# The first stage's projection on eight 64x32 tiles, its gram on column halves and its gate on four strips at once

## The chip, the cores and the metric

One Trainium2 chip, of which the kernel uses one core. The metric is the device time of one execution in microseconds (us), from start to end on the chip.

## The reference

Two layers work on an image x of 4 x 64 x 256 x 256 (batch, channels, height, width), all in fp32. Layer 0 is a channel-attention block with a convolutional feed-forward part; layer 1 is a linear attention along rows, one along columns and a two-layer perceptron. The change touches the start of layer 0 only. Cut to that:

```python
h = layernorm(x, ln1_w, ln1_b)              # over the 64 channels of a pixel
proj = conv1x1(h, in_proj_w)                # 64 -> 64 channels
local, glob = split(proj, 2, axis=1)        # 32 + 32 channels
qkv = dwconv3x3(conv1x1(glob, qkv_w), qkv_dw)
q, k, v = split(qkv, 3)                     # 4 heads of 8 channels each
g = sigmoid(conv1x1(relu(conv1x1(glob, gate_w1, gate_b1)), gate_w2, gate_b2))
dk = clip(floor(8 * g.mean()), 1, 8)        # one number from all pixels
attn = einsum(l2norm(q), l2norm(k))         # 8 x 8 per head, summed over all pixels
attn = softmax(where(attn >= kth_largest(attn, dk), attn, -inf))
```

So the stage needs three things of every pixel: its projection (kept for later), its share of the products of q and k (the gram, summed over all pixels of an image) and its gate value (summed over everything). The local half goes on to a branch of its own (`_lgce` in the reference: a 1x1 convolution, a channel weight from the image's means, and two sigmoids).

## The kernel before

The kernel is one program written in stages, and every engine runs its instructions in the order of the program. The stage that is changed, `stage_a`, walks over 4 images of 16 strips; a strip is 16 image rows, and a pass of the loop over n is called a step here. A step works on several strips at once, through generators that `_steps` advances in turn: `pairs` for strip n-3, `proj` for strip n-1, `norm` for strip n, and in every second step of images 1 to 3 also `local` for the image before. `gate` runs ahead of them, for strip n-2.

- `norm` transposes the strip on PE from channels on partitions to pixels on partitions (L520), ACT copies that out of PSUM into `xp` (L521), and `layernorm` (L311 to L321) runs on DVE and ACT: a sum, a subtraction, a square on ACT (L314), a sum, a square root on ACT (L318), a reciprocal, a product.
- `proj` transposes the result back (L540, copied out on DVE at L541), so that 128 partitions hold the 64 channels of an even and of an odd row ("parity"), and multiplies by `win` (L547), a 128x128 matrix that has the 64x64 weights of either parity on its diagonal and zeros elsewhere. ACT adds the bias and writes `pj` (L549), which goes to DRAM (L556). The gate's hidden layer follows, on four tiles of 32 columns (L559), with its relu on DVE (L561).
- `pairs` brings `pj` into `gp`, four image rows on 128 partitions, by SBUF-to-SBUF DMAs (L577 to L585), convolves to q and k of two rows at once by three accumulated matmuls (L604), DVE copies that into `qT` (L609), and the gram adds qT times qT (L595, 128x128, of which only the two 64x64 blocks on the diagonal are read, at L637 and L638).
- `gate` multiplies the hidden layer of one strip by the second gate weights (L566), and ACT takes the sigmoid and its sum (L568).
- `local` is two groups of 32x32 tiles (L462), ACT evictions (L466, L470), a product on DVE (L472) and a sigmoid on ACT (L473).

An fp32 matmul of the source stands in the trace as two LDWEIGHTS and two MATMULs. Tiles of PSUM come from `mm()`, a ring of six banks that all parts of the stage share in the order of the program; the gram has one of two `sm()` banks. ACT must load a table when it changes between sigmoid (L470, L473, L568) and square root (L318).

The constants come from `_prep` as packs, one DMA each: pack "a" has `win`, `g2T` (second gate weights, one 16x8 matrix per strip part, of which 8 columns are used) and their biases. After stage_a come the last image's `local`, the attention weights, and the later stages, which the change does not touch.

Of the kernel before, what the change touches and what calls it, by code (L numbers as in the profile page):

```python
# [22 lines left out]
def _prep(a):  # L23
# [7 lines left out]
    def put(name, v, rows=None):  # L31
        v = np.asarray(v, f)
        P[name] = grp, v.reshape(v.shape[0] if rows is None else rows, -1)
# [8 lines left out]
    def col(v, n):  # L42
        return np.tile(np.asarray(v).reshape(-1), n)[:, None]
# [14 lines left out]
    for par in (0, 1):  # L58
        for lg in (0, 1):
            win[par, :, lg, par, :] = wi[lg * 32:(lg + 1) * 32].T  # L60
    put("win", win, 128)
    put("ln1w", col(L0["ln1_w"], 2))
    put("ln1b", col(L0["ln1_b"], 2))
    qkv, dwq = L0["qkv_w"], L0["qkv_dw"][:, 0]
# [16 lines left out]
        g1[64 + par * 32:96 + par * 32, par, :] = L0["gate_w1"].T  # L81
    put("g1T", g1)
    put("g1b", col(L0["gate_b1"], 8))
    g2 = np.zeros((8, 16, 8), f)
    for i in range(8):
        g2[i, :, i] = L0["gate_w2"][0]
    put("g2T", g2, 128)
    put("g2b", col(L0["gate_b2"], 8))


    grp = "l"
# [4 lines left out]
    put("spb", col(np.repeat(L0["cbam_spb"][:, 0], 4), 4))  # L96
    put("gmask", p[:, None] % 32 // 4 == p[None, :] % 32 // 4)
    grp = "s"
    put("ones8", np.ones((8, 32)))
    put("fold", (p[:, None] % 64 == np.arange(64)[None, :]))  # L100
    put("hb", (p[:32, None] // 8 == p[None, :32] // 8))
    put("vA", qkv[64:])
# [145 lines left out]
def kernel(ctx: ExitStack, tc: tile.TileContext, x, packs, fd, out, off):  # L248
# [77 lines left out]
    p1 = sp1.enter_context(tc.tile_pool(name="pst1", bufs=1))  # L326
    KL = load_pack(p1, "l")
    sumA = p1.tile([128, B], F32, name="sumA")
    gsum = p1.tile([8, B, 16], F32, name="gsum")
    gram2 = [p1.tile([128, 64], F32, name=f"gram{b}") for b in range(B)]  # L330
    wc = [const.tile([128, 3, 64], F32, name=f"wc{b}") for b in range(B)]
    cw = [p1.tile([128, 1], F32, name=f"cw{b}") for b in range(B)]
# [10 lines left out]
    def attention_weights():  # L343
        vt = p1.tile([32, 12, 32], F32, name="vt")
        V.tensor_tensor(vt, mid_bc(K("vA"), 12), bc(K("vD"), 32), ALU.mult)

        gs = p.tile([8, 1], F32, name="gs")
        V.tensor_reduce(gs, gsum.rearrange("p a b -> p (a b)"), AX.X, ALU.add)
        t = mm()
        T.matmul(t[:32, 0:1], K("ones8"), gs, start=True, stop=True)  # L350
        dk = p1.tile([32, 1], F32, name="dk")
        V.tensor_scalar(dk, t[:32, 0:1], 8.0 / (B * HW), 1.0, ALU.mult, ALU.max)
        asc = p1.tile([32, 1], F32, name="asc")
        V.tensor_reduce(asc, K("asc"), AX.X, ALU.add)
        for b in range(B):

            t = mm()
            T.matmul(t[:64, :64], K("fold"), gram2[b], start=True, stop=True)
            gm = p.tile([64, 64], F32, name="gm")
            V.tensor_copy(gm, t[:64, :64])  # L360
            dg = p.tile([64, 64], F32, name="dg")
            V.tensor_tensor(dg, gm, ident[:64, :64], ALU.mult)
            n2 = p.tile([64, 1], F32, name="n2")
            V.tensor_reduce(n2, dg, AX.X, ALU.add)
            nr = p.tile([64, 1], F32, name="nr")
            V.tensor_scalar(n2, n2, 1e-24, None, ALU.max)
            S.activation(nr, n2, AF.Sqrt)
            ri = p.tile([64, 1], F32, name="ri")
            V.reciprocal(ri, nr)
            n1 = p.tile([64, 64], F32, name="n1")  # L370
            V.tensor_scalar(n1, gm, ri, None, ALU.mult)
            t = mm()
            T.transpose(t[:64, :64], n1, ident[:64, :64])
            nn = p.tile([64, 64], F32, name="nn")
            V.tensor_scalar(nn, t[:64, :64], ri, None, ALU.mult)
            am = p.tile([32, 32], F32, name="am")
            V.tensor_tensor(am, nn[0:32, 32:64], K("hb"), ALU.mult)
            at = p.tile([32, 8], F32, name="at")
            V.tensor_reduce(at, am.rearrange("p (h d) -> p d h", h=4), AX.X, ALU.add)
            V.tensor_scalar(at, at, K("temp"), None, ALU.mult)  # L380

            gt = p.tile([32, 8, 8], F32, name="gt")
            V.tensor_tensor(gt, mid_bc(at, 8), bc(at, 8), ALU.is_gt)
            kp = p.tile([32, 8], F32, name="kp")
            V.tensor_reduce(kp, gt, AX.X, ALU.add)
            V.tensor_scalar(kp, kp, 1.0, dk, ALU.add, ALU.is_le)
            mx = p.tile([32, 1], F32, name="mx")
            V.tensor_reduce(mx, at, AX.X, ALU.max)
            V.tensor_scalar(at, at, mx, None, ALU.subtract)
            ex = p.tile([32, 8], F32, name="ex")  # L390
            S.activation(ex, at, AF.Exp)
            V.tensor_tensor(ex, ex, kp, ALU.mult)
            sx = p.tile([32, 1], F32, name="sx")
            V.tensor_reduce(sx, ex, AX.X, ALU.add)
            rx = p.tile([32, 1], F32, name="rx")
            V.reciprocal(rx, sx)
            V.tensor_scalar(ex, ex, rx, asc, ALU.mult, ALU.mult)
            pb = p.tile([32, 4, 8], F32, name="pb")
            V.tensor_tensor(pb, mid_bc(ex, 4), K("hb").rearrange("p (h d) -> p h d", h=4), ALU.mult)

            t = mm()
            T.matmul(t[:32, :64], pb.rearrange("p h d -> p (h d)"), K("opgT"), start=True, stop=True)
            eb = p.tile([32, 64], F32, name="eb")
            V.tensor_copy(eb, t[:32, :64])
            t = mm()
            for i in range(3):
                T.matmul(t[:, i * 64:(i + 1) * 64], vt[:, i * 4:(i + 1) * 4, :].rearrange("p a c -> p (a c)"), eb, start=True, stop=True)
            V.tensor_copy(wc[b].rearrange("p a c -> p (a c)"), t[:, :192])

            V.tensor_copy(wc[b][64:96, 1, :], K("oplr")[64:96])  # L410
            yield
# [74 lines left out]
    def stage_a():  # L486
        NS = H // 16
        with tc.tile_pool(name="pa", bufs=2) as pa, tc.tile_pool(name="pa1", bufs=1) as pk:
            K = load_pack(pk, "a")

            win = pk.tile([128, 128], F32, name="win")
            V.tensor_scalar(win, K("win"), K("ln1w"), None, ALU.mult)
            t = mm()
            T.matmul(t[:, 0:1], K("win"), K("ln1b"), start=True, stop=True)
            bin_ = pk.tile([128, 1], F32, name="bin_")
# [14 lines left out]
            def norm(b, s):  # L510

                xs = ld.pop((b, s))
                xns[b, s] = []
                for hf in (0, 1):
                    xp = pa.tile([128, 16, C], F32, name="xp")
                    for k in (0, 1):
                        tp = mm()
                        for i in range(4):
                            ii = hf * 8 + k * 4 + i
                            T.transpose(tp[:, i * 128:(i + 1) * 128], xs[:, ii // 2, (ii % 2) * 128:(ii % 2) * 128 + 128], ident)  # L520
                        S.copy(xp[:, k * 8:(k + 1) * 8, :].rearrange("p a c -> p (a c)"), tp)  # L521
                    yield
                    xn = pa.tile([128, 16, C], F32, name="xn", bufs=4)
                    layernorm(pa, xp, xn, 16)
                    xns[b, s].append(xn)
                    yield

            def proj(b, s):
# [13 lines left out]
                    xTs.append(xT)  # L542
                    yield
                for hf in (0, 1):
                    for k in (0, 1):
                        pr = mm()
                        T.matmul(pr, win, xTs[hf][:, k * 512:(k + 1) * 512], start=True, stop=True)  # L547
                        n = (s * 2 + hf) * 2 + k
                        S.activation(pj[:, hf * 4 + k * 2:hf * 4 + k * 2 + 2, :].rearrange("p a c -> p (a c)"), pr, AF.Identity,  # L549
                                     bias=bin_, accum_out=sacc[b][:, n:n + 1])  # L550
                    yield
# [5 lines left out]
                hp = mm()  # L557
                for i in range(4):
                    T.matmul(hp[i * 32:(i + 1) * 32, :], K("g1T"), pj[:, 2 * i:2 * i + 2, :].rearrange("p a c -> p (a c)"), start=True, stop=True)  # L559
                hs = pa.tile([128, 512], F32, name="hs")  # L560
                V.tensor_scalar(hs, hp, K("g1b"), 0.0, ALU.add, ALU.max)  # L561
                hss[b, s] = hs

            def gate(b, s):
                zp = mm()
                T.matmul(zp[:8, :], K("g2T"), hss.pop((b, s)), start=True, stop=True)  # L566
                gj = pa.tile([8, 512], F32, name="gj")
                S.activation(gj, zp[:8, :], AF.Sigmoid, bias=K("g2b"), accum_out=gsum[:, b, s:s + 1])  # L568

            def pairs(b, s):  # L570

# [20 lines left out]

                def acc(qT, i):
                    for k in range(4):
                        T.matmul(gram[:, :128], qT[:, k * 128:(k + 1) * 128], qT[:, k * 128:(k + 1) * 128],  # L595
                                 start=(s == 0 and i == 0 and k == 0), stop=(s == NS - 1 and i == 3 and k == 3))

                for i in range(4):
                    yield
# [17 lines left out]
            for n in range(len(seq) + 3):  # L617
                if n + 1 < len(seq):
                    ld[seq[n + 1]] = load(*seq[n + 1])
                if 0 <= n - 2 < len(seq):  # L620
                    gate(*seq[n - 2])

                m = n - NS - 2
# [10 lines left out]
                    local_weights(b)  # L634
                if n >= 3 and seq[n - 3][1] == NS - 1:
                    b = seq[n - 3][0]
                    V.tensor_copy(gram2[b][0:64], grams[b][0:64, 0:64])  # L637
                    V.tensor_copy(gram2[b][64:128], grams[b][64:128, 64:128])  # L638

    stage_a()  # L640

# [713 lines left out]
```

## Time and profile before

| | |
|---|---|
| median of 3 runs | 9063.34 us (9060.01 to 9071.98) |
| the profiled execution | 9063.4 us, span 9061.6 us |
| PE busy over the span | 8382.1 us (93%) |
| DVE, ACT busy | 5945.5 us (66%), 4740.4 us (52%) |
| stage_a's gram, L595 | 2048 MATMULs, busy 287.9 us |
| stage_a's projection, L547 | 512 MATMULs, busy 242.1 us |
| stage_a's gate, L566 | 128 MATMULs, busy 79.6 us |
| stage_a's convolution, L604 | 6144 MATMULs, busy 733.3 us |
| table loads of L568 and L318 in stage_a and just after | 60 and 87, of 1283 ns each |

Busy time is the union of the instructions of a row, and [...] consecutive matmuls overlap. The time from the start of one group of instructions to the start of the next says more about what the engine can do; the timeline view gives it. A row of the timeline has the start, the length, the engine, the line, the operation with its tiles and shapes, and in brackets the idle time before it and what ended that.

### The profile page before, as it was taken

The page shows a single profiled execution, that of the slowest core. Times are in us where ns is not written, and L with a number is a line of the kernel's source. Part 1 is how long each engine was busy: PE and PEld are TensorE (multiplying, and loading weights), DVE is VectorE, ACT ScalarE, POOL GpSimd, SP SyncE. Part 2 cuts the span into 40 slices and gives each one's busy share as a digit, 9 for nine tenths or more (in the row PEclk, how much of TensorE's full clock was granted, in tenths as well). Part 3 has the DMA queues.
Part 4 walks back from the last instruction along what each step waited for, and adds up shares of the span by engine and source line. Part 5 has one row for each costly group of instructions (what it writes and reads, how often), then busy time and mean ns, then how long its engine had stood idle before and what let it go on. Part 6 is the DMA issues. An engine that isn't in the chain of part 4 may idle for free. (4 is left out here: it accounts for less than half of the span.)

```text
span 9061.6 us, 136047 instructions
## 1 busy us (share of the span) xinstructions
PE 8382.1 (93%) x53934; PEld 4354.5 (48%) x53934; DVE 5945.5 (66%) x8509; ACT 4740.4 (52%) x7844; POOL 1135.0 (13%) x1828
## 2 busy tenths in 40 slices
PE   8999999789999998999999999999997888898897
PEld 7877777534444443333333344444453333333333
DVE  6666666467777775222222288888887778878876
ACT  4455555545555554222222266666655767766765
POOL 1111111112221221000000011111110000000000
PEclk9999999889999999999999999999998999999999
DMA  6677767599999998888888855555533233233232
GB/s 149 138 178 173 173 168 172 152 317 384 391 393 392 382 388 333 297 297 296 297 297 297 279 163 172 173 172 168 168 117 69 53 66 66 55 66 64 58 66 47
DMA packets 1258475, 1831.95 MB, mean 202 GB/s; under 512 B 335600, under 2 KB 1040112, under 8 KB 1196656
## 3 DMA queue, kind: packets, MB, share of 16 engines
q1 hardware_dynamic: 1053296, 1034.55, 37.8%
q0 software_dynamic: 204544, 788.69, 26.6%
q8 instruction: 428, 7.01, 0.3%
q14 instruction: 207, 1.70, 0.1%
HBM read 967.57 MB, written 788.53 MB: 194 GB/s over the span
## 5 line engine op out<-in xcount | busy, mean ns | idle before, releaser
L900 DVE TENSOR_TENSOR y<-ge,mm 128x512 f32<-128x512 f32 (+1 forms) x640 | 406.2, 635 | 1212.2 <-ACT ge L899 1212.2
L867 PE MATMUL mm<-t,w 128*128 128x512 f32 (+1 forms) x2560 | 1093.9, 566 | 19.6 <-DMA t<-td 19.6
L899 ACT ACTIVATE ge<-mm 128x512 f32<-128x512 f32 (+1 forms) x640 | 354.7, 554 | 1253.8 <-PE mm L874 1253.8
L1298 ACT ACTIVATE hg<-mm,b 128x512 f32<-128x512 f32 x1024 | 631.7, 685 | 332.6 <-PE mm L1296 330.7
L760 PE MATMUL mm<-gp,wc 128*64 128x510 f32 (+1 forms) x3072 | 702.0, 595 | 89.4 <-DVE xm L770 51.2
L867 PEld LDWEIGHTS mm<-t,w 128*128 128x128 f32 x2560 | 455.4, 190 | 648.1 <-issue 437.5
L604 PEld LDWEIGHTS mm<-wqk,gp 128*128 128x128 f32 x6144 | 711.6, 192 | 71.2 <-issue 42.4
L604 PE MATMUL mm<-wqk,gp 128*128 128x128 f32 x6144 | 733.3, 276 | 0.0
L1307 PE MATMUL mm<-hg,pack_d 128*64 128x512 f32 x2048 | 579.4, 609 | 100.7 <-ACT hg L1298 100.7
L1296 PE MATMUL mm<-xfT,w 64*128 64x512 f32 x2048 | 638.4, 666 | 4.8 <-ACT xfT L1285 4.2
L815 ACT COPY tb<-mm 128x512 f32<-128x512 f32 x512 | 300.2, 587 | 632.3 <-PE mm L809 632.0
L874 PE MATMUL mm<-t,w 64*64 64x504 f32 (+1 forms) x5120 | 575.6, 555 | 0.0
L809 PE MATMUL mm<-xl,pack_c 64*128 64x512 f32 x2048 | 511.8, 599 | 8.9 <-ACT xl L797 4.7
L760 PEld LDWEIGHTS mm<-gp,wc 128*64 128x64 f32 x3072 | 278.1, 137 | 468.0 <-issue 330.2
L314 ACT ACTIVATE ln_sq<-xn 128x1024 f32<-128x1024 f32 x256 | 274.4, 1072 | 347.1 <-DVE xn L312 347.0
L316 DVE TENSOR_REDUCE ln_v<-ln_sq 128x16 f32<-128x1024 f32 x256 | 311.9, 1219 | 147.2 <-ACT ln_sq L314 147.2
L955 PE MATMUL mm<-ya,pack_e 128*64 128x512 f32 x1024 | 381.1, 616 | 11.2 <-DMA ya<-yd 11.2
L1309 DVE TENSOR_SCALAR st<-mm,pack_d 128x512 f32<-128x512 f32 x256 | 279.1, 1090 | 169.8 <-PE mm L1307 169.8
L1167 ACT ACTIVATE ln_sq<-xc 128x1024 f32<-128x1024 f32 x256 | 266.9, 1055 | 219.9 <-DVE xc L1165 219.7
L813 DVE COPY tb<-mm 128x512 f32<-128x512 f32 x512 | 344.9, 685 | 22.3 <-PE mm L809 16.8
L1296 PEld LDWEIGHTS mm<-xfT,w 64*128 64x128 f32 x2048 | 220.9, 202 | 272.4 <-issue 159.5
L874 PEld LDWEIGHTS mm<-t,w 64*64 64x64 f32 x5120 | 158.1, 132 | 374.4 <-issue 374.4
(455 smaller groups left out, 15547.3 us busy)
## 6 DMA issues: line engine op xcount, KB each, us to landing
t<-td SPq DMA_DIRECT2D x256, 1152.0 KB, 10.5
td<-tb POOLq DMA_DIRECT2D x144, 1024.0 KB, 16.1
td<-tb POOLq DMA_DIRECT2D x288, 512.0 KB, 13.9
yd<-y POOLq DMA_DIRECT2D x128, 1152.0 KB, 10.1
ya<-yd SPq DMA_DIRECT2D x192, 512.0 KB, 5.7
xs<-in_x_dram SPq DMA_DIRECT2D x128, 512.0 KB, 6.7
projd<-pj POOLq DMA_DIRECT2D x256, 256.0 KB, 4.8
gp<-projd SPq DMA_DIRECT2D x128, 512.0 KB, 9.5
```

Source lines behind the costliest of these rows:

```text
L604: T.matmul(qp[:, k * 128:(k + 1) * 128], gp[:, 2 * i + k // 2, at + dx:at + dx + 128], wqk[:, dx, :], start=(dx == 0), stop=(dx == 2))
L760: T.matmul(tv[i * 64:(i + 1) * 64, :, o], wc[2 * pr + i][:, dx, :], gps[i][:, 2 * r:2 * r + 2, i_], start=(dx == 1), stop=False, skip_grou ...
L809: T.matmul(t, inT[q, hf * 128:(hf + 1) * 128], xls[b // 2, s][q, :, 2 * y:2 * y + 2].rearrange("p f y t -> p f (y t)"), start=True, stop=True)
L813: V.tensor_copy(o, i_)
L867: T.matmul(t[:, :n], w[:, 0:128], x_[:, c, :], start=True, stop=False, skip_group_check=True)
L874: T.matmul(t[po:po + 64, :n].rearrange("p (n c) -> p n c", c=64)[:, :, o], w[q:q + 64, 128:192], x_[q:q + 64, c, i_], start=False, stop=Tr ...
L899: S.activation(ge[:, :n], ts[0][k][:, :n], AF.Gelu)
L900: V.tensor_tensor(y[:, c, :].rearrange("p n c -> p (n c)"), ge[:, :n], ts[1][k][:, :n], ALU.mult)
L955: T.matmul(t[b * 64:(b + 1) * 64, :], owT, ya[:, :, 2 * r:2 * r + 2, b * 64:(b + 1) * 64].rearrange("p f y t -> p y f t"), start=True, sto ...
L1296: T.matmul(t, w1[rh * 64:(rh + 1) * 64, i * 128:(i + 1) * 128], xT[rh * 64:(rh + 1) * 64], start=True, stop=True)
L1298: S.activation(g, t, AF.Gelu, bias=b1[:, i:i + 1])
L1307: T.matmul(y[rh * 64:(rh + 1) * 64, :], w2[:, i, :], hg[i * 2 + rh], start=False, stop=(i == 1), skip_group_check=True)
```

## The change

The projection no longer multiplies by zeros. For each half strip the two banks of PSUM (k = 0, 1) are filled together by eight matmuls, each of 64 rows by 32 columns: row half r of `xT` with the weights of that parity, for the local and the global channels (lg). For the second bank the column place of the two parities is swapped, so that the eight tiles lie in eight different places of the array; to have the right parity there, `norm` writes the second half of `xp` with the two parities exchanged, by two copies in place of one. The gram is computed as two products of 64 columns, which go to partitions 0 to 63 and 64 to 127 of the same bank. The gate waits until four strips have their hidden layers and runs their four matmuls at once, each with 32 columns of weights (24 of them zero), then one sigmoid over 128 partitions.

The line attention of layer 1 is the same in both kernels.

```diff
     put("win", win, 128)
+    put("winx", win[::-1], 128)
...
-    g2 = np.zeros((8, 16, 8), f)
+    g2 = np.zeros((8, 16, 32), f)
...
-    put("g2b", col(L0["gate_b2"], 8))
+    put("g2b", col(L0["gate_b2"], 128))
...
-    put("ones8", np.ones((8, 32)))
+    put("ones8", np.tile(p[:, None] % 32 < 8, (1, 32)))
...
-    gsum = p1.tile([8, B, 16], F32, name="gsum")
+    gsum = p1.tile([128, B, 4], F32, name="gsum")
...
+            winx = pk.tile([128, 128], F32, name="winx")
+            V.tensor_scalar(winx, K("winx"), K("ln1w"), None, ALU.mult)
...
-                        S.copy(xp[:, k * 8:(k + 1) * 8, :].rearrange("p a c -> p (a c)"), tp)
+                        if k == 0:
+                            S.copy(xp[:, 0:8, :].rearrange("p a c -> p (a c)"), tp)
+                        else:
+                            for a in (0, 1):
+                                S.copy(xp[:, 8:16, :].rearrange("p (i a) c -> p a i c", a=2)[:, 1 - a], tp.rearrange("p (i a c) -> p a i c", a=2, c=C)[:, a])
...
                 for hf in (0, 1):
-                    for k in (0, 1):
-                        pr = mm()
-                        T.matmul(pr, win, xTs[hf][:, k * 512:(k + 1) * 512], start=True, stop=True)
+                    prs = [mm(), mm()]
+                    for lg in (0, 1):
+                        for r in (0, 1):
+                            for k, w in ((0, win), (1, winx)):
+                                q = lg * 64 + (r ^ k) * 32
+                                T.matmul(prs[k][q:q + 32, :], w[r * 64:(r + 1) * 64, q:q + 32], xTs[hf][r * 64:(r + 1) * 64, k * 512:(k + 1) * 512], start=True, stop=True)
+                    for k, pr in enumerate(prs):
...
-                hs = pa.tile([128, 512], F32, name="hs")
+                hs = pa.tile([128, 512], F32, name="hs", bufs=5)
...
             def gate(b, s):
                 zp = mm()
-                T.matmul(zp[:8, :], K("g2T"), hss.pop((b, s)), start=True, stop=True)
-                gj = pa.tile([8, 512], F32, name="gj")
-                S.activation(gj, zp[:8, :], AF.Sigmoid, bias=K("g2b"), accum_out=gsum[:, b, s:s + 1])
+                for i in range(4):
+                    T.matmul(zp[i * 32:(i + 1) * 32, :], K("g2T"), hss.pop((b, s - 3 + i)), start=True, stop=True)
+                gj = pa.tile([128, 512], F32, name="gj", bufs=1)
+                S.activation(gj, zp, AF.Sigmoid, bias=K("g2b"), accum_out=gsum[:, b, s // 4:s // 4 + 1])
...
                     for k in range(4):
-                        T.matmul(gram[:, :128], qT[:, k * 128:(k + 1) * 128], qT[:, k * 128:(k + 1) * 128],
-                                 start=(s == 0 and i == 0 and k == 0), stop=(s == NS - 1 and i == 3 and k == 3))
+                        for po in (0, 1):
+                            v = qT[:, k * 128 + po * 64:k * 128 + po * 64 + 64]
+                            T.matmul(gram[po * 64:po * 64 + 64, :64], v, v, start=(s == 0 and i == 0 and k == 0), stop=(s == NS - 1 and i == 3 and k == 3))
...
-                if 0 <= n - 2 < len(seq):
+                if 0 <= n - 2 < len(seq) and n % 4 == 1:
                     gate(*seq[n - 2])
...
-                    V.tensor_copy(gram2[b][0:64], grams[b][0:64, 0:64])
-                    V.tensor_copy(gram2[b][64:128], grams[b][64:128, 64:128])
+                    V.tensor_copy(gram2[b], grams[b][:, 0:64])
```

More of the change, by code (lines that the diff above doesn't have):

```diff
@@ L345, in attention_weights @@
         V.tensor_tensor(vt, mid_bc(K("vA"), 12), bc(K("vD"), 32), ALU.mult)
-        gs = p.tile([8, 1], F32, name="gs")
+        gs = p.tile([128, 1], F32, name="gs")
         V.tensor_reduce(gs, gsum.rearrange("p a b -> p (a b)"), AX.X, ALU.add)
```

## The prediction

> **What bounds the kernel now.** The page first: PE is busy for 93% of the span, and the slices put the changed stage, stage_a, into the first eight of forty, with PE at 8 or 9 tenths. Then the timeline of all engines in that stage. One step (16 image rows) starts with the transposes of line L540. In the first batch each step takes 23.5 us: L540 starts at 151.04 and again at 174.56. From L462's first use on, steps alternate, one with a piece of local() and one without; a pair takes about 54.9 us (L540 at 876.54 and 931.38). The windows of two plain steps, of a step with local() and of the 4 us after it:
>
> ```profile
> core 0: us, PE busy (x) PEld busy (x) DVE busy (x) ACT busy (x) POOL busy (x), PEclk, DMA share, GB/s
> 111.00:134.50 23.50, 23.50 (x180) 19.60 (x180) 15.90 (x21) 10.99 (x21) 2.48 (x6) 1.00 0.68 146
> 134.50:158.00 23.50, 23.50 (x180) 19.60 (x180) 15.90 (x21) 10.98 (x21) 2.47 (x6) 1.00 0.70 146
> 876.40:903.90 27.50, 25.47 (x233) 19.42 (x232) 17.07 (x19) 20.18 (x32) 6.84 (x14) 1.00 0.78 204
> 903.90:907.90 4.00, 3.59 (x11) 1.93 (x11) 1.02 (x2) 0.00 (x0) 0.00 (x0) 0.57 1.02 269
> ```
>
> A plain step is PE from end to end. A step with local() is not: ACT has 20 us of 27.5, and the timeline at its end shows PE waiting for DVE, which follows ACT:
>
> ```profile
> 901.02 1.06 PE L559 MATMUL mm<-pj,pack_a 128*32 128x512 f32 x8
> 901.80 0.31 ACT L318 ACTIVATE ln_d<-ln_v,eps_t 128x16 f32<-128x16 f32 x1
> 902.43 1.23 DVE L321 TENSOR_TENSOR xn<-xn,ln_r 128x1024 f32<-128x1024 f32 x1
> 903.57 0.68 DVE L609 COPY qT<-mm 128x512 f32<-128x512 f32 x1
> 904.31 2.08 PE L595 MATMUL sm<-qT 128*128 128x128 f32 x8 [2.23 <-DVE qT L609]
> 906.32 1.61 PE L566 MATMUL mm<-hs,pack_a 128*8 128x512 f32 x2
> ```
>
> After that wait of 2.23 us the granted clock falls (0.57 in the last window; L595's eight take 2.08 instead of 1.06 us). PE's own rows give the prices, start to start:
>
> ```profile
> 159.08 1.06 PE L595 MATMUL sm<-qT 128*128 128x128 f32 x8
> 159.97 1.88 PE L547 MATMUL mm<-xT,win 128*128 128x512 f32 x4
> 161.69 1.04 PE L520 MATMUL mm<-pack_k,xs 128*128 128x128 f32 x8
> ...
> 170.53 1.06 PE L595 MATMUL sm<-qT 128*128 128x128 f32 x8
> 171.52 1.07 PE L559 MATMUL mm<-pj,pack_a 128*32 128x512 f32 x8
> 172.52 1.16 PE L595 MATMUL sm<-qT 128*128 128x128 f32 x8
> 173.60 1.02 PE L566 MATMUL mm<-hs,pack_a 128*8 128x512 f32 x2
> 174.56 1.09 PE L540 MATMUL mm<-pack_k,xn 128*128 128x128 f32 x8
> ```
>
> Each matmul of the source stands twice (two passes). A whole-array pass of 512 columns costs (161.69 - 159.97)/4 = 0.43 us, one of 128 columns 0.89/8 = 0.11. L559 is four tiles of 32 columns side by side: its eight instructions take 1.00, little more than two passes. L595 before it takes 0.99 in place of 0.89: 0.10 for the change of tile shape; L566 to L540 has it too (0.96 = 0.86 + 0.10).
>
> [...]
>
> ```profile
> L1064 PE MATMUL sm<-xe,kx 128*32 128x64 f32 x4096 | 73.0, 225 | 43.0 <-ACT kx L1043 43.0
> ```
> [...] the 60 loads of L568 take 1283 ns each.
>
> **The change, part by part, in PE time of one step (64 steps).**
> - Projection, L547: 8 whole-array passes, 8 x 0.43 = 3.44. Now twice eight 64x32 tiles, which fill the array: two passes each, 0.86, and 0.07 for sixteen starts, so 1.86. Saves 1.58. Bounds: L462's 32x32 tiles, 24 in 1.15 us, show small tiles packing; from 1.4 to 1.7.
> - Gram, L595: 32 x 0.11 = 3.58. Now 64 instructions on two halves. No row has 64 columns of weights with 64 moving. Twice L1064's 18 ns (two tiles, not four) is 36 ns; a quarter of 112 is 28. I take 29: 16 in 0.47 us, four groups 1.88. Saves 1.70. If halves do not overlap, each costs 56 and it saves nothing.
> - Gate, L566: 0.86 in each step, now four tiles at once in one step of four, 0.91/4 = 0.23. Saves 0.63.
> - Mode changes: 4 in a step (into and out of L559, into and out of L566); now 10.25 (gram, projection and L559 each have their own shape), 6.25 x 0.093 = 0.58 added.
> Sum: 3.3 us a step, **213 us** in all if nothing but PE counted.
>
> Off PE: ACT loses 48 gates of 0.68 + 0.19 and, by the order of the two kernels' instructions, 94 table loads (568 to 474), 47 of them before L318: near 160 us of ACT work, mostly beside PE. It gains a copy per half: the second 128x512 copy of L521 becomes two of 128x256. From 128x512 at 588 and L314's 128x1024 at 1060 ns, 256 columns are 352 ns: 2 x 352 - 588 = +0.12 us, twice a step, on the path that feeds DVE (no row has copies in such pieces: between nothing, where they overlap, and 0.3). One DVE copy per batch and a wider constant pack cost under 1 us together. SP, POOL and the DMAs issue the same work in the same order; the share of 0.68 to 0.78 would rise to 0.8 or 0.85. gp is filled a step ahead (issued 900.56, read 934.5), so that is hidden. After stage_a every engine's list of instructions is the same.
>
> New waits: PE's gate in every fourth step waits for hs of the step just ended (L561), with L540 queued behind; before, it did so in every step. The second projection bank must be free 0.86 us earlier than now; it is the buffer of six allocations before, evicted microseconds earlier.
>
> **What the other engines give back.** A plain step: both banks of the first projection are now ready together, near 160.85, so ACT's two L549 end at 162.2 rather than 162.57 and the second half's L521 starts only 0.35 us sooner. From there the chain L521, L311, L312, L314, L316, L318, L320, L321 takes what it took (8.0 us to 170.6 before), plus 0.12; L609 then adds 0.65 and L595 0.55: the next L540 at about 171.55. Step 20.5 instead of 23.5; with a gate (1.0) every fourth step, 20.75. Saves **2.75**.
>
> A pair with local(): from L521 (878.16) to the last qT (904.25) the 26.1 us run over ACT and DVE; PE's saving does not shorten them. Where no gate precedes, the table load of the first L318 goes (0.6 us of the path), 0.3 on average; the copies add 0.2: 26.0. Then L595 0.55, gate 0.5 on average, L540 and L520 1.6, and 1.7 for a window of half clock, since PE now waits longer there, near 2.8 us; then a plain step of 20.5. Sum 50.9 against 54.9. Five of the 24 pairs lost no clock and stand at 53.3, so the average before is 54.5: saves **3.7**.
>
> Sum: 16 x 2.75 + 24 x 3.7 = 44 + 89 = **133 us**. The profiled execution took 9063.4 us (span 9061.6 and 1.8 around it), the median of the runs shown is 9063.34. So **8930 us**. What tells a change from none is about 0.2%, 18 us.
>
> **The rivals.**
> - PE bounds all of it: the chain slides along with PE. -213, **8850**. For it: the plain steps at 23.50 of 23.50. Against: 2.23 us of wait each pair.
> - Steps with local() give nothing and plain ones 2.0: 40 x 2.0 = 80, **8983**. For it: ACT's 20 us.
> - The half clock spreads: waits as long as 2.2 us come into every step, each giving back 1.7 us, 64 x 1.7 = 109: 24 us remain, **9040**; against: plain steps show no gap from which it would grow.
> - Slower: the gram's halves neither overlap nor shorten, weights of 64 columns costing each instruction the 0.11 us of a whole one. Then 256 groups take 1.79 instead of 0.47, +338: 213 - 338, **9188**. It decides from 81 ns an instruction ((0.47 + 213/256)/16). Against: L1064, and PEld of 64 columns at 135 ns in L1307's row against 192.
>
> **How the numbers follow.** Main case 0.72 (own range 8875 to 8995), all-PE 0.10, nothing in local() 0.09, half clock 0.05, serial gram 0.04. The range 8855 to 8998 leaves out the last two, and half of all-PE. Faster by over 0.2%: 0.93; within: 0.03; slower: 0.04.
>
> **What would show it.** In the changed kernel: plain steps near 20.5 us; projection groups of 16 in about 0.95 us and gram groups of 16 in 0.5; L318's table loads at 40 and the gate's at 12; PE waiting near 2.8 us for qT ahead of the last gram of a step with local(), and the half clock behind it; the last gate (1698 us now) near 1565. It is wrong if gram groups take 0.9 us or more, if plain steps stay over 22, or if anything after stage_a changes its length.

## The result, and the profile after

The changed kernel takes **8941.27 us** (median of 4 runs, 8937.15 to 8942.61); the kernel before took 9064.61 beside it (4 runs). The ratio is 0.9862, 95% interval 0.9845 to 0.9879: faster by 123 us, where 133 was forecast. The profiled execution took 8937.15 us, with a span of 8935.4.

The last gate, which ends the stage for this purpose, starts at 1571.96 us and started at 1698.44 before; the spans differ by 126.2, so all of the gain lies ahead of it. The first lines of the page of the kernel after:

```profile
span 8935.4 us, 143218 instructions
## 1 busy us (share of the span) xinstructions
PE 8237.0 (92%) x57518; PEld 4221.3 (47%) x57518; DVE 5940.4 (66%) x8506; ACT 4587.6 (51%) x7782; POOL 1133.1 (13%) x1828
```

PE has 145 us less of busy time, and the program became 126 us shorter: part of what PE saved went into waiting. The windows of the kernel after, two plain steps and then three stretches of images 1 to 3, beside which local() runs in every second step:

```profile
core 0: us, PE busy (x) PEld busy (x) DVE busy (x) ACT busy (x) POOL busy (x), PEclk, DMA share, GB/s
111.00:131.50 20.50, 20.31 (x240) 17.05 (x232) 15.85 (x20) 7.65 (x19) 2.47 (x6) 1.00 0.85 183
131.50:152.00 20.50, 20.30 (x240) 17.06 (x232) 15.84 (x20) 7.65 (x19) 2.47 (x6) 1.00 0.74 154
875.00:902.90 27.90, 25.43 (x274) 19.19 (x273) 19.48 (x24) 11.15 (x25) 4.85 (x12) 0.94 0.70 175
903.00:932.30 29.30, 27.19 (x297) 20.21 (x297) 17.02 (x20) 17.18 (x30) 6.50 (x12) 0.88 0.86 196
932.30:958.00 25.70, 23.80 (x248) 19.37 (x247) 17.32 (x21) 9.53 (x20) 2.72 (x9) 0.93 0.70 170
```

A plain step is 20.5 us, with PE busy for 20.3 of them. In each of the other three, PE is idle for about 2 us and its clock is at 0.88 to 0.94 of full speed. From start to start of the groups of the gate's hidden layer (L572 after, L559 before), plain steps alternate as 20.5, 20.5, 20.5, 21.6, the last with the gate in it; the pairs of a step with and one without local() average 51.5 us over 22 pairs, and 54.8 before.

The new operations on PE, from the timeline of PE in a plain step of the kernel after:

```profile
162.74 2.84 PE L620 MATMUL mm<-wqk,gp 128*128 128x128 f32 x24
165.51 0.69 PE L612 MATMUL sm<-qT 128*64 128x64 f32 x16
166.12 0.61 PE L559 MATMUL mm<-xT,win 64*32 64x512 f32 x1
166.13 0.61 PE L559 MATMUL mm<-xT,winx 64*32 64x512 f32 x1
...
167.14 1.09 PE L524 MATMUL mm<-pack_k,xs 128*128 128x128 f32 x8
```

The gram's sixteen instructions (L612) take 0.61 us to the start of the projection, 0.15 of it the gap between the two tile shapes; so 29 ns each. The projection's sixteen (L559) start about 7 ns apart, eight at a time, and take 1.02 us with a change of shape in it. On ACT, the groups of the stage, forms kept apart:

```profile
L530 ACT COPY xp<-mm 128x256 f32<-128x256 f32 x256 | 84.1, 388 | 1.2 <-PE mm L524 1.2
L527 ACT COPY xp<-mm 128x512 f32<-128x512 f32 x128 | 74.7, 583 | 181.1 <-PE mm L524 181.1
L320 ACT ACT_TABLE_LOAD x40 | 51.3, 1283 | 0.7
L583 ACT ACT_TABLE_LOAD x12 | 15.4, 1283 | 0.2
```

The square root has 40 table loads left and the gate 12, as foreseen.

What was not foreseen is where PE waits. These are PE's waits for qT in the stage, up to the last gate: what waited, for what, us in total, times, longest. First the kernel before, then the kernel after.

```profile
PE sm L595 <- DVE qT L609: 50.6, 23, 2.2
PE mm L462 <- DVE qT L609: 4.9, 23, 0.2
```
```profile
PE sm L612 <- DVE qT L625: 46.9, 41, 2.5
PE mm L464 <- DVE qT L625: 29.2, 23, 2.1
```

Before, the long waits, of 2.2 us, stood once in a pair, ahead of the last gram of the step with local(). After, by the timeline, 31 waits are longer than 1.5 us: 12 ahead of the second group of local() (L464), and 19 ahead of grams, all of them in steps without local(). Where the long wait stood before, ahead of the last gram of a step with local(), none is longer than 0.2 us. The timeline of PE after has one long wait in either kind of step, and between them (931.63) the last gram of the step with local(), without one:

```profile
913.10 1.93 PE L464 MATMUL mm<-L,spw 32*32 32x512 f32 x8 [2.11 <-DVE qT L625]
914.96 5.28 PE L620 MATMUL mm<-wqk,gp 128*128 128x128 f32 x24
...
930.64 1.07 PE L572 MATMUL mm<-pj,pack_a 128*32 128x512 f32 x8
931.63 0.69 PE L612 MATMUL sm<-qT 128*64 128x64 f32 x16
...
942.35 0.69 PE L612 MATMUL sm<-qT 128*64 128x64 f32 x16 [1.90 <-DVE qT L625]
```

The convolution behind the first (L620) takes 5.28 us instead of 2.84: half clock (from 913.07 to 919.90 the trace has it at 0.50, and a pass of the convolution takes 213 ns instead of 112). Between 60 us and the last gate the trace has the clock at one half for 64.8 us before and for 116.2 after.

Why qT is late shows on DVE. Its timeline in a step without local(), in the kernel before:

```profile
911.79 1.23 DVE L312 SCALAR_TENSOR_TENSOR xn<-ln_s,xp 128x1024 f32<-128x1024 f32 x1
912.93 0.69 DVE L609 COPY qT<-mm 128x512 f32<-128x512 f32 x1
913.53 1.28 DVE L541 COPY xT<-mm 128x512 f32<-128x512 f32 x2
914.72 1.21 DVE L316 TENSOR_REDUCE ln_v<-ln_sq 128x16 f32<-128x1024 f32 x1
```

and in one of the kernel after:

```profile
936.24 1.22 DVE L314 SCALAR_TENSOR_TENSOR xn<-ln_s,xp 128x1024 f32<-128x1024 f32 x1
938.58 1.22 DVE L318 TENSOR_REDUCE ln_v<-ln_sq 128x16 f32<-128x1024 f32 x1 [1.12 <-ACT ln_sq L316]
940.18 0.25 DVE L322 RECIPROCAL ln_r<-ln_d 128x16 f32<-128x16 f32 x1 [0.38 <-ACT ln_d L320]
940.47 1.23 DVE L323 TENSOR_TENSOR xn<-xn,ln_r 128x1024 f32<-128x1024 f32 x1
941.61 0.68 DVE L625 COPY qT<-mm 128x512 f32<-128x512 f32 x1
```

Before, the copy of qT came ahead of the rest of the layer norm and filled the time that DVE would have spent waiting for ACT's square. After, it stands behind the whole layer norm, and DVE idles 1.12 us for the square and 0.38 for the square root with that copy queued behind it. Counted over DVE's instructions in the trace, no step of the kernel before, from the first local() on, has this copy behind the whole layer norm of the first half; in the kernel after 32 have it (20 without local(), 12 with it), and 31 of these are the ones with a long wait.

The new order also took a wait away. In a step with local(), the last copy of qT stood before behind the product of the second half's layer norm (the prediction's lines at 902.43 and 903.57); after, it stands ahead of the reciprocal:

```profile
930.13 0.69 DVE L625 COPY qT<-mm 128x512 f32<-128x512 f32 x1 [0.34 <-PE mm L620]
931.52 0.25 DVE L322 RECIPROCAL ln_r<-ln_d 128x16 f32<-128x16 f32 x1 [0.70 <-ACT ln_d L320]
```

No line of the diff touches this order. Nor is it the order of the program, as the section on the kernel before has it: the source writes a layer norm in one piece, and in both traces copies of qT and xT stand between its instructions. The program's scheduler, which settles each engine's queue when the kernel is built, has put the queue together anew inside images 1 to 3.

### The profile page after: what moved, and what is told of

The parts are those of the page before. It is cut to its first block, busy times and chain, and to the rows that moved or that the text cites. A ratio compares the mean times of both kernels' runs of the same rounds, so it can differ in the third digit from the quotient of the medians.

```text
span 8935.4 us, 143218 instructions
## 1 busy us (share of the span) xinstructions
PE 8237.0 (92%) x57518; PEld 4221.3 (47%) x57518; DVE 5940.4 (66%) x8506; ACT 4587.6 (51%) x7782; POOL 1133.1 (13%) x1828
## 5 line engine op out<-in xcount | busy, mean ns | idle before, releaser
L620 PEld LDWEIGHTS mm<-wqk,gp 128*128 128x128 f32 x6144 | 728.0, 197 | 99.0 <-issue 60.7
L620 PE MATMUL mm<-wqk,gp 128*128 128x128 f32 x6144 | 761.5, 282 | 1.1 <-POOL gp L589 0.9
```

Of the source, the lines that this page charges most:

```text
L620: T.matmul(qp[:, k * 128:(k + 1) * 128], gp[:, 2 * i + k // 2, at + dx:at + dx + 128], wqk[:, dx, :], start=(dx == 0), stop=(dx == 2))
```

## The experiments

In each comparison "before" is the kernel before on the same chip; its medians are 9061.47 to 9066.22. The chip differs between groups of experiments, so that a difference between two changed kernels, taken from their medians, is good to a few us only. How good shows in what lies behind the last gate: all but the two kernels that move work there do nearly the same there, and their profiled executions took 7355.7 to 7371.7 us for it. So the time of the last gate is given too where it matters. Line numbers shift by a few between kernels; the tiles' names stay.

**One part at a time.** Three kernels have one part of the diff each, with nothing else changed: the projection with its exchanged parities, the gram on halves, the gate on four strips.

```diff
# the gram alone
-  T.matmul(gram[:, :128], qT[:, k * 128:(k + 1) * 128], qT[:, k * 128:(k + 1) * 128], ...)
+  for po in (0, 1):
+      v = qT[:, k * 128 + po * 64:k * 128 + po * 64 + 64]
+      T.matmul(gram[po * 64:po * 64 + 64, :64], v, v, ...)
```

Projection alone: 

> The kernel before with the projection on eight tiles alone (with the exchanged copies and the second weight matrix). By PE's account 1.58 us a step less four changes of shape (0.37): 1.2 us, 77 us in all, if PE is all that counts. Theory (the chain over ACT and DVE holds the steps with local()): plain steps gain 1.1 us (23.5 to 22.4), a pair with local() only about 1.1 in all, so about 45 us. Rival (PE counts alone): 77 us.

Gram alone: 

> The kernel before with the gram on column halves alone. 1.70 us a step less five changes of shape (0.47): 1.23 us, 79 us if PE is all that counts. Theory (chain): plain steps 23.5 to 22.3, a pair with local() 1.2 less in all, so about 50 us. Rival (PE alone): 79 us. If column halves did not run side by side: no gain, or a loss of up to 30 us from the changes of shape.

Gate alone: 

> The kernel before with the gate of four strips at once alone. PE: 0.63 and 1.5 changes of shape fewer (0.14), 0.77 us a step, 49 us. On ACT some 95 table loads fewer, of which half of the steps with local() feel 0.6 us on the chain. Theory (chain): plain steps 0.77 less on average, pairs 1.3 less, about 43 us. Rival (PE alone): 49 us. Together with the two others the theory expects about 140 us, somewhat more than the whole change gave (123), since whatever comes first uses up the slack.

Measured: the projection alone 9039.81 against 9066.22, ratio 0.9969 (0.9957 to 0.9980), -26 us; the gram alone 9068.00, 1.0003 (0.9995 to 1.0011), nothing; the gate alone 9034.36, 0.9964 (0.9950 to 0.9978), -32. Together -57, where the whole change gives -123. Each gave less than its theory and its rival had (45 or 77, 50 or 79, 43 or 49 us). Plain steps became shorter in all three: to 22.5, 23.0 and 22.4 (23.6 with the gate); only the gram's stayed clearly behind what was expected (22.3). No gain is also what halves that do not run side by side would have given; but they do in this kernel too, at 29 ns an instruction. What was lost shows in the waits of PE. With the projection alone:

```profile
PE sm L607 <- DVE qT L621: 40.2, 21, 1.9
PE mm L578 <- DVE hs L573: 38.8, 23, 1.7
```

and with the gram alone:

```profile
PE mm L566 <- DVE hs L561: 54.4, 58, 1.9
PE sm L597 <- DVE qT L610: 35.5, 20, 1.9
```

The gate on one strip now waits for hs, the hidden layer that DVE has just made, 39 and 54 us in all; neither the kernel before nor the whole change has this wait, the latter since the gate on four strips comes once in four steps. It is the old wait in a new place. With either part, DVE's order is new in much the same way as in the whole change. The wait ahead of the last gram of a step with local() is gone, and the gate behind that gram waits in its stead, for hs, which DVE makes behind the same layer norm. With the gram alone PE waits even less for qT than before (40.5 against 55.5 us). So the parts are not additive: the gate's part also takes away a wait that the other two make. Of the gram's saving on PE (by the prediction's prices 1.70 us a step less five changes of shape of 0.093, so 79 us in all) nothing is left in the sum.

**Is it local()?** The prediction had a step with local() held by 26 us over ACT and DVE. In two kernels all of local() is taken out of the loop and runs behind the stage, for before and for after.

```diff
-  if m >= 0 and lb < B - 1 and li % 2 == 0: local_load(lb, li // 2)
   _steps(*(f(*seq[n - d]) for d, f in ((3, pairs), (1, proj), (0, norm)) if 0 <= n - d < len(seq)),
-         local(lb, li // 2) if m >= 0 and lb < B - 1 and li % 2 == 1 else None)
...
-  b = B - 1
-  (load, local and local_end of b)
+  for b in range(B):
+      (load, local and local_end of b)
```

Before, local() behind the stage: 

> The kernel before with all of local() taken out of stage_a and run behind it, with the last image's. All 64 steps should be plain, 23.5 us each; local() behind the stage costs about 11 us a piece for 24 pieces, against 7.9 us a pair inside: about 75 us slower than before, 9140 us. It is the base of the next kernel only.

After, the same: 

> The changed kernel with all of local() behind stage_a in the same way. Theory (local()'s chain over ACT and DVE, with the half clock behind it, is where the gain is lost): without it all steps are plain, 20.5 and 21.6 us, and the change is worth 64 x 2.75 = 176 us against the kernel with local() behind and without the change. Rival (the plain steps lose as much as those with local()): the change stays worth about 125 us.

Measured: 9114.54 against 9062.61, ratio 1.0055 (1.0042 to 1.0067), for before (52 us slower, where 75 were expected); 8947.16, 0.9870 (0.9855 to 0.9885), for after. The difference of the two is 167 us: what the change saves where every step is plain. All steps are now 23.5 in the one and 20.5 or 21.6 in the other, in all four images. The timeline of PE in image 2 of the second, from one hidden layer of the gate to the next (20.48 us):

```profile
704.59 1.06 PE L572 MATMUL mm<-pj,pack_a 128*32 128x512 f32 x8
...
725.07 1.06 PE L572 MATMUL mm<-pj,pack_a 128*32 128x512 f32 x8
```

The last gate moved from 1528.92 to 1355.43 us, by 173, close to the theory's 176; behind the stage 7 us are lost again. So the plain step's 2.75 us hold for all 64 steps, and what is given back, 44 of the 167 us (47 of 173 by the last gates), is given back only where local() runs in the loop.

**local() spread over two steps.** If the length of local() in one step is what gives back, half of it in each step should help after more than before. Its first half (the group with the layer's weights and the sigmoid) stays; the second (L464's second group, the product, the last sigmoid) moves to the next step.

```diff
-  local(lb, li // 2) if m >= 0 and lb < B - 1 and li % 2 == 1 else None)
+  local_pre(lb, li // 2) if m >= 0 and lb < B - 1 and li % 2 == 1 else None,
+  local_sw((m - 1) // NS, (m - 1) % NS // 2) if m >= 1 and (m - 1) // NS < B - 1 and li % 2 == 0 else None)
```

Before, spread: 

> The kernel before with local() spread over two steps: its first half (pre) in the odd step, its second half (sw and the sigmoid) in the next. No work is added or left out. Theory (the chain of ACT and DVE in the step with local() binds): a pair becomes PE again, 2 x 23.5 and 2.4 us for the two groups of L462, 49.4 against 54.5, so 120 us faster, about 8940. Rival (the pair costs what local()'s work costs wherever it stands): no change.

After, spread: 

> The changed kernel with local() spread over two steps in the same way. Theory: a pair falls from 51.5 to about 44 to 46 us, some 130 to 170 us faster than the changed kernel, about 8790; the change is then worth 150 to 170 us between the two kernels with local() spread. Rival (ACT and DVE hold every step by their work alone): half of that, about 8870.

Measured: 9012.46, ratio 0.9944 (0.9931 to 0.9956), for before; 8880.03, 0.9797 (0.9783 to 0.9810), for after. Spreading gave 50 and 61 us, half or less of what the theory had (120, and 130 to 170), and nearly the same to both; the second is near its rival's 8870. With local() spread the change is worth 132 us, not 150 to 170. Spreading helps, but it isn't where the change's gain went. What was left in the second kernel is a wait, on PE and then on DVE:

```profile
920.06 1.12 PE L618 MATMUL sm<-qT 128*64 128x64 f32 x16 [5.21 <-DVE qT L631]
```
```profile
914.12 1.21 DVE L318 TENSOR_REDUCE ln_v<-ln_sq 128x16 f32<-128x1024 f32 x1
917.89 0.25 DVE L322 RECIPROCAL ln_r<-ln_d 128x16 f32<-128x16 f32 x1 [2.56 <-ACT ln_d L320]
918.18 1.22 DVE L323 TENSOR_TENSOR xn<-xn,ln_r 128x1024 f32<-128x1024 f32 x1
919.32 0.68 DVE L631 COPY qT<-mm 128x512 f32<-128x512 f32 x1
```

Here the copy of qT is queued behind a reciprocal that waits 2.56 us for ACT. This points to the order on DVE rather than to the length of local(); the last three kernels test it.

**Is it the half clock?** A kernel gives PE work that nothing needs, the gate's hidden layer three times over in the steps with local(): if the clock falls for want of work there, this should cost little or even gain.

```diff
-  for i in range(4):
+  for i in range(4 * (1 + 2 * extra[0])):      # extra[0] is 1 in a step with local()
+      i %= 4
       T.matmul(...)                             # the hidden layer, L572
```

> The changed kernel with the four tiles of the gate's hidden layer (the same result) computed three times over in the 24 steps with local(), ahead of the last gram, where PE waits. It adds 1.8 us of PE work to each of these steps. Theory (the idle wait costs a window of half clock behind it): with PE busy through the wait the clock stays up in the step that follows, 1.7 us for each pair, so 20 to 40 us faster than the changed kernel though there is more work. Rival (the clock's drop costs nothing that counts): the same, or up to 43 us slower (24 x 1.8).

Measured: 8970.11 against 9061.47, ratio 0.9898 (0.9882 to 0.9915), 29 us slower than the kernel after, where the theory had 20 to 40 faster. The added work is two more groups in each of 24 steps, 24 x 1.8 = 43 us of PE time, and most of it is paid. The waits stay where they were: in one step with local(), 2.10 us ahead of L464's second group, and the convolution behind it took 5.49. The trace has the clock at one half for 113 us, against 116. The idle time doesn't stand where the work was added, which is ahead of a gram that no longer waits. This speaks against the cure, not against the half clock as a cost.

**The exchange of parities.** The second half of xp in one copy of 512 columns, as before. This kernel leaves the exchange out, so its projection of that half is another result; it serves for the time alone:

```diff
-  if k == 0: S.copy(xp[:, 0:8, :]..., tp)
-  else: (two copies of 256 columns, parities exchanged)
+  S.copy(xp[:, k * 8:(k + 1) * 8, :].rearrange("p a c -> p (a c)"), tp)
```

> The changed kernel with the second half of xp copied in one piece as before, so that the two parities are not exchanged there (that part of the computation is changed). Theory: the exchange costs 0.12 us twice a step on the chain, 8 to 15 us in all. Rival: it is hidden, under 3 us.

Measured: 8932.11, ratio 0.9854 (0.9839 to 0.9869), 9 us faster than the kernel after (6 when each is held against the kernel before beside it, and the intervals of the two ratios overlap); a plain step is 20.4. The last gate came only 2.0 us earlier, at 1569.98 for 1571.96; the rest lies behind the stage, where the two kernels are alike. By the rows ACT is busy with the three copies of a half for at most 1.24 us (74.7 + 84.1, over 128 halves), and with the two here for 1.08 (138.0 over 128): of the 0.16, times 128 = 20 us, little reaches the time. The rival, that the exchange is hidden (under 3 us), fits the stage better than the theory's 8 to 15.

**An edge in the order on DVE.** One edge is added: the reciprocal of the layer norm (L322) may not be queued ahead of the newest copy of qT. That fills DVE's wait for the square root with that copy, and takes no work away. It is not quite the order of the kernel before, in which the copy stood ahead of the second sum.

```diff
-  def layernorm(pool, src, xc, g, bufs=None):
+  def layernorm(pool, src, xc, g, bufs=None, behind=None):
...
-      V.reciprocal(s4, s3)
+      with tc.issue_after(behind) if behind is not None else ExitStack():
+          V.reciprocal(s4, s3)
...
-  layernorm(pa, xp, xn, 16)
+  layernorm(pa, xp, xn, 16, behind=last.get("qT"))
...
-  V.tensor_copy(qT, qp)
+  last["qT"] = V.tensor_copy(qT, qp).ins
```

On the kernel after: 

> The changed kernel with one more rule of order for VectorE: the reciprocal of each layer norm in stage_a is queued behind the newest qT copy. The planner had put that copy behind the whole layer norm of the first half in most steps of images 1 to 3, where the kernel before has it ahead. Nothing is added but the order. Theory (the place of the qT copy in DVE's queue took the pairs' gain: PE waits about 2 us for it twice in a pair, with the half clock behind each wait): a pair falls from 51.5 us to 48 to 50, so 35 to 80 us faster than the changed kernel, about 8885. Rival (the chain of local() over ACT and DVE holds the pair whatever DVE's order): within 10 us of the changed kernel.

On the kernel with the gram alone: 

> The gram on column halves alone, with the same rule of order. Theory (the halves alone gave nothing because DVE's queue was ordered anew): pairs fall from 55.1 to about 53, so 40 to 60 us faster than the gram alone, about 9020. Rival: no change, about 9068.

On the kernel after with local() spread: 

> The changed kernel with local() spread over two steps and the same rule of order. Theory: pairs of steps fall from 48.7 to about 45 to 46, so 60 to 90 us faster than with local() spread alone, about 8805. Rival: no change, 8880.

Measured, against 9063.17: 8844.52, ratio 0.9761 (0.9748 to 0.9775), **97 us faster than the kernel after**; 8991.51, 0.9922 (0.9910 to 0.9935), 77 faster than the gram alone; 8801.25, 0.9711 (0.9698 to 0.9724), 79 faster than the spread without the edge, and 262 faster than the kernel before: the best of all. Held against the kernel before on its own chip, each gain is 95, 73 and 79 us; by the last gates, 86, 64 and 76. The first two are above what the theory had (35 to 80, 40 to 60), the third within it, and the rivals, which had no change, are out. DVE's timeline in the first, with the copy where it fills the wait:

```profile
900.10 1.22 DVE L318 TENSOR_REDUCE ln_v<-ln_sq 128x16 f32<-128x1024 f32 x1 [1.12 <-ACT ln_sq L316]
901.24 0.68 DVE L627 COPY qT<-mm 128x512 f32<-128x512 f32 x1
901.83 1.28 DVE L552 COPY xT<-mm 128x512 f32<-128x512 f32 x2
903.03 0.24 DVE L323 RECIPROCAL ln_r<-ln_d 128x16 f32<-128x16 f32 x1
```

PE's waits of that kernel in the stage, to be held against those of the kernel after:

```profile
PE sm L614 <- DVE qT L627: 18.4, 57, 0.7
PE mm L465 <- DVE qT L627: 6.5, 23, 0.4
```

The waits for qT that are left are at most 0.7 us long. The whole stage in one window, for the kernels before and after and for the kernel with the edge; the columns are those of the windows above:

```profile
60.00:1698.40 1638.40, 1576.93 (x12501) 1250.66 (x12499) 1035.54 (x1237) 885.59 (x1507) 255.31 (x560) 0.98 0.69 164
```
```profile
60.00:1572.00 1512.00, 1427.91 (x15942) 1116.93 (x15943) 1028.36 (x1230) 736.65 (x1444) 253.37 (x560) 0.96 0.76 177
```
```profile
60.00:1486.40 1426.40, 1393.71 (x15963) 1085.55 (x15961) 1024.08 (x1234) 733.08 (x1444) 253.39 (x560) 1.00 0.80 188
```

The clock column went from 0.98 to 0.96 with the change, and to 1.00 with the edge. In the trace the half clock lasts 3.4 us in the last, against 116.2. The waits for qT fall from 76.1 to 24.9 us, and a us at half clock loses half a us of PE work (213 ns a pass instead of 112): 51 + 0.5 x 113 = 108 at most, as an estimate, since part of the half clock falls into the waits themselves; the stage became 86 us shorter, the program 97. The pairs average 47.6 us.

The edge gives 97, 77 and 79 us on three kernels that differ in the projection, the gate and the place of local(). With the gram alone it takes the waits for qT from 40.5 us to 5.0 and leaves those of the gate for hs (54.2).

The edge was not tried on the kernel before. There the first copy stands ahead of the first half's reciprocal in every step already, so that only the wait at the last gram of a step with local() (50.6 us in all) could change, and that wait may only move to the gate, as it did with the gram alone. What the edge would give there is not known.

## Why the prediction was right, and where not

- **A plain step, 20.5 for 23.5**: right, 20.5 (21.6 with the gate), and 167 us (173 up to the last gate) over 64 steps in the pair of kernels without local() in the loop, where 64 x 2.75 is 176.
- **Sizes on PE**: right. A gram group has 29 ns an instruction (16 in 0.47 us, as taken), a projection group 0.93 for its passes and 0.09 for a change of shape, 1.02 us together. The 29 was the author's estimate, from the row of L1064 (73.0 us for 4096, 18 ns each) and from a quarter of 112. The rival of a serial gram, which needed over 81 ns, is out. The two halves of the gram run side by side: the second starts 7 ns after the first, and a pair of them takes 58 ns where one whole-array pass took 112.
- **Copies and tables**: the copies of 256 columns take 388 ns where 352 was estimated, but a pair overlaps and takes 0.66 us where 0.70 was reckoned; what one copy in place of two saves is 9 us at most, and 2 by the last gate. The table loads are at 40 and 12.
- **Nothing after the stage**: right. From the last gate to the end, 7363 us in both.
- **A pair with local()**: the size was near (saved 3.3 us, from 54.8 to 51.5, against 3.7), the reason was wrong, so the near size is luck. The step that failed reads "from L521 (878.16) to the last qT (904.25) the 26.1 us run over ACT and DVE; PE's saving does not shorten them". They do get shorter: with the edge the same pairs take 47.6 us, with all of local() still in its place. What held the step was DVE's queue, in which qT stood behind a layer norm that waits for ACT; so it was in the kernel before already, in the very lines that the prediction shows.
- **Where PE waits**: wrong. The prediction had 2.8 us ahead of the last gram of a step with local(), once in a pair. At that place 0.2 us at most are left. In place of 23 long waits there are 31, of up to 2.5 us, at L464's second group and in steps without local(). Half clock does follow most of them (27 of the 31), as said: 116 us of it against 65.
- **The order**: the prediction compared the engines' lists after the stage, found them alike, and took the order of DVE inside a step as unchanged. That was the hidden assumption under the two points above.
- **The sum**: 133 was forecast, 123 measured. The pairs' miss of 0.4 us in each of 24 accounts for 10 us. The prediction has 176 us for plain steps all through and gives 43 of them back in the pairs (176 less 133); measured are 167 and 44. So both terms are near, the second by luck: the prediction gives the 43 back to a fixed chain with one longer wait at its end. The traces have in its place, at other points, 20.6 us more of waiting for qT and 51 us more at half clock: by estimate 20.6 + 51/2 = 46 us. The rival in which PE bounds all of it had 8850; the kernel with the edge reaches 8844.52, though by another sum, since it also lacks waits that the kernel before had (55.5 us for qT and 64.8 at half clock, of which 24.9 and 3.4 are left).

The three kernels with the edge show that the place of one copy on DVE costs these kernels 73 to 97 us, and the long waits stand in just the steps in which that place is new. How much of this is a loss against the kernel before is not measured, since the edge was not tried there; the 46 us are an estimate from the traces. Why the scheduler chose that order isn't shown either: the change altered the instructions of PE and ACT around it, and the gram alone was enough to bring it about in steps without local(). That it comes from the shorter time of PE in the scheduler's own reckoning is only argued.

## What to carry to other kernels

When a change makes one engine's work shorter, compare the order of all engines' queues inside the changed stage, not only behind it: a scheduler may put them together anew, and a copy that another engine waits for may come to stand behind an instruction that itself waits. Look on the late engine's timeline for an idle gap with a ready instruction queued behind it; an edge in the program's order that fills the gap was worth 97 us here, nearly as much as the change. And test the parts of a change together as well as alone: alone they gave 57 of 123 us, and the projection and the gram alone each met a wait at the gate that the third part removes.

## What was not expected of the hardware

A wait of about 2 us was enough for half clock: 2.11 us ahead of L464, and the convolution behind it took 5.28 us instead of 2.84. In the stage of the kernel after, no wait of PE is longer than 2.5 us. Of its 31 pieces at half clock 27 last 3.41 us and four last twice that; a piece of 3.41 us costs 1.7 us of PE work by estimate (half of it), as much as the prediction took, whose window of 4.00 us at 0.57 gives 1.72. A wait of this length is not always followed by one: in the kernel before 5 of 23 were not, and with the gram and the edge 18 of 23 waits of 1.6 to 1.9 us for hs were not. With waits for qT of 0.7 us at most, one piece of 3.4 us was left in 1426, behind another wait, of 1.3 us. What decides whether a wait is followed by half clock is not shown.
